# One layer's context products: a single run of tiled products per block, at another place in the block, with another cut of the features

## The chip, the cores and the metric

The kernel runs on one core of one Trainium2 chip. Times are device microseconds (us) of that core. "The trace" is the record of one profiled execution; "the page" is its summary. A stage's length below is read from the trace, from the start of the stage's first matmul to the start of the next stage's first.

## The reference, cut to what matters

128 sequences of 64 tokens with 768 features, two layers:

```python
h = jnp.maximum(_layernorm(x), 0.0)
for l in range(2):
    m_left  = einsum('bsh,oh->bso', h, W_left[l])       # pass one
    m_right = einsum('bsh,oh->bso', h, W_right[l])
    u       = ...                                       # scores from h, m_left, m_right, masked
    attention = exp(u) * adj / row sums
    h_lin = einsum('bsh,oh->bso', h, W_lin[l]) + b_lin[l]   # pass two
    ctx   = attention @ h_lin                               # the "context": 64x64 times 64x768
    h     = relu(layer_norm(ctx))
return x + h
```

Everything is in float32. In the trace each matmul of a product is two records on TensorE (the 8 matmuls of a context run, below, are 16 records).

## The kernel before: the parts concerned

Each layer has two passes over 16 blocks of 512 tokens (8 sequences). Pass one makes scores and attention. Pass two makes `h_lin` of block `u` as 15 products (ORDER has 15 entries; each product is 8 records of 256 columns), and, between two of them, the context of block `u-1`. A context product is 64x64, so four of them run at once on four quarters of TensorE ("tiled form"; in the trace the four start 6.6 ns apart). Results of products go to PSUM, the memory that TensorE writes; X, Y, Z, V and the two halves of each "aux" tile are its banks, of 512 columns each. `put(n, f)` sets step `f` of another engine into slot `n`; each product has two slots, in its middle and at its end.

```python
def context(u, r):                                   # half a block: 4 sequences
    cx = [ps_aux.tile([P, 2, T], F32, name="aux") for _ in range(2)]
    for n in range(2):
        for (j, k, i) in ((lo, 0, lo), (hi, 0, hi), (lo, 1, hi), (hi, 1, lo)):
            q = r + 2 * k
            m = n if j == lo else 1 - n              # the four tiles write four banks
            nc.tensor.matmul(cx[k][i, m, :HH], at[j, q, :], hl[j, q, m * HH:(m + 1) * HH], ...)
    return [c[:, :, :HH] for c in cx]                # HH = 384

def linear(u, rs, base, ends, more):
    for i, (s, at, t, _) in enumerate(ORDER):        # the 15 products
        ... matmuls into bank X, Y, Z or V; read(p, ...) by ScalarE or VectorE
        if i == 11 and more:
            AHEAD.append(fresh(l, 0, more))          # X for the next block, preloaded by ScalarE
        if i in ends:                                # a context run stands after product i
            what, slots = ends[i]
            for f, n in zip(finish(*what), slots):   # context + its layer norm, in later slots
                put(n, f)
...
if u:
    ends = {0: ((u - 1, 0), (6, 7, 8, 11, 12)), 7: ((u - 1, 1), (20, 21, 22, 30, 30))}
```

So before, the context of a block is two runs, after product index 0 and index 7 (the first and the eighth product), each of 8 matmuls of 384 columns (16 records). `finish` squares the context on ScalarE, then scales it by the inverse deviation; the last block of a layer works with half-width products (4 records).

## Time and profile before

| | before |
|---|---|
| time, median of 3 (range) | 2761.79 us (2761.58 to 2762.23) |
| span of the profiled execution | 2758.5 us |
| first layer: pass one, pass two | 897.49, 470.95 us |
| second layer: pass one, pass two to the end | 896.51, 480.21 us |
| period of a block in pass two, blocks 1 to 14 of both layers | 29.196 or 29.197 us (29.27 in block 1 of the second layer) |

The page, its chain and the blocks of pass two are shown in the prediction. This row of the page's costliest groups is every context record of the kernel (after the shapes: count, busy us, mean ns of one, idle time before):

```profile
L642 PE MATMUL aux<-hl,at 64*64 64x384 f32 x1024 | 99.2, 495 | 0.0
```

1024 records in groups of 16 are 64 runs: 32 blocks, two runs each. And these are four products of the last block of the first layer, TensorE in order of time (start, length by modelled ends, what; in brackets the idle time before it and who ended it):

```profile
1369.86 1.13 PE L758 MATMUL V<-w_n,ht 128*128 128x256 f32 x4
1370.83 1.03 PE L758 MATMUL X<-w_n,ts 128*128 128x256 f32 x4
1371.69 1.03 PE L758 MATMUL Y<-w_n,ts 128*128 128x256 f32 x4
1373.18 1.13 PE L758 MATMUL X<-w_n,ht 128*128 128x256 f32 x4 [0.47 <-ACT hl L200]
```

A product of four records normally takes 0.863 us from start to start (1370.83 to 1371.69). The one at 1371.69 takes 1.49: the next product waits for ScalarE to read a bank.

### The profile page before, as it was taken

The numbers are of one execution on the slowest core, as the hardware profiler recorded it, in microseconds if no ns is written. First come the engines' busy times: TensorE is split into PE (matmuls) and PEld (weight loads), VectorE is DVE, ScalarE is ACT, GpSimd is POOL, SyncE is SP. The second block draws the span as 40 slices with busy tenths as digits, with TensorE's granted clock in tenths as the row PEclk, the third lists the DMA queues.
The fourth block names the chain that finished last, engine by engine and source line by source line (L and its number), as shares of the span: only waits on it lengthen the run. The fifth ranks groups of instructions, "written<-read, shape, count | busy, mean of one in ns | idle before, by whom it ended". The sixth has DMA issues, their size and how long they took to land.

```text
span 2758.5 us, 46190 instructions
## 1 busy us (share of the span) xinstructions
PE 2731.5 (99%) x18712; PEld 2336.8 (85%) x18712; DVE 1333.8 (48%) x2255; ACT 842.3 (31%) x1469; POOL 1191.2 (43%) x935
## 2 busy tenths in 40 slices
PE   8999999999999999999999999999999999999998
PEld 7888888888888888888788888888888888888886
DVE  6555445544453322323335444443444335666667
ACT  3222223222321244444521211222121214544443
POOL 3332442223223465565422344223222335887886
PEclk9999999999999999999999999999999999999999
DMA  6424433343231343443545422443234204555555
GB/s 203 121 75 103 118 79 81 98 122 80 75 90 62 96 136 108 127 142 100 152 126 154 100 75 76 106 120 79 75 96 118 63 26 147 159 172 164 169 167 145
DMA packets 234070, 310.80 MB, mean 113 GB/s; under 512 B 54146, under 2 KB 184450, under 8 KB 225666
## 3 DMA queue, kind: packets, MB, share of 16 engines
q1 hardware_dynamic: 233698, 307.45, 40.3%
q8 instruction: 149, 2.44, 0.4%
q14 instruction: 63, 0.52, 0.1%
q10 hardware_dynamic: 160, 0.39, 0.0%
HBM read 202.91 MB, written 104.86 MB: 112 GB/s over the span
## 4 chain that ended last, share of the span: by engine, by line
PE 97%; DVE 1%; DMA 1%; ACT 0%; issue 0%; SPq 0%; DVEq 0%; ACTq 0%
PE X L422 23%; PE V L422 16%; PE X L758 12%; PE Y L422 12%; PE Z L422 8%; PE V L758 8%; PE Y L758 6%; PE aux L449 5%; PE Z L758 4%; PE aux L642 3%; DVE wm L463 0%; DMA w_l<-in_w_left_dram 0%; DMA w_r<-in_w_right_dram 0%; DVE w_l L155 0%; DVE w_r L155 0%
## 5 line engine op out<-in xcount | busy, mean ns | idle before, releaser
L155 POOL TENSOR_TENSOR ts<-ht 128x512 f32<-128x512 f32 x441 | 585.8, 1340 | 1218.3 <-DMA ht<-h 461.1
L200 ACT ACTIVATE m<-X 128x512 f32<-128x512 f32 (+1 forms) x256 | 151.6, 592 | 1101.0 <-PE X L422 583.7
L155 POOL TENSOR_TENSOR ts<-ht,ts 128x512 f32<-128x512 f32 x189 | 249.2, 1326 | 151.2 <-PE X L758 75.6
L155 DVE TENSOR_TENSOR m<-m,V 128x512 f32<-128x512 f32 (+1 forms) x256 | 173.3, 677 | 270.4 <-PE V L422 270.2
L155 DVE TENSOR_TENSOR m<-m,X 128x512 f32<-128x512 f32 (+1 forms) x256 | 162.9, 677 | 249.2 <-PE X L422 248.5
L758 PE MATMUL X<-w_n,ts 128*128 128x256 f32 x1024 | 244.1, 380 | 0.8 <-ACT hl L200 0.6
L422 PE MATMUL X<-ts,w_l 128*128 128x256 f32 x1024 | 242.7, 380 | 1.2 <-DVE ts L155 0.6
L422 PE MATMUL X<-ts,w_r 128*128 128x252 f32 (+1 forms) x1024 | 238.7, 376 | 0.0
L155 DVE TENSOR_TENSOR m<-m,Z 128x512 f32<-128x512 f32 (+1 forms) x128 | 87.4, 683 | 306.1 <-ACT m L200 246.6
L758 PEld LDWEIGHTS X<-w_n,ts 128*128 128x128 f32 x1024 | 191.6, 190 | 32.2 <-issue 2.3
L422 PEld LDWEIGHTS X<-ts,w_l 128*128 128x128 f32 x1024 | 192.0, 190 | 31.5 <-DVE m L155 2.7
L422 PEld LDWEIGHTS X<-ts,w_r 128*128 128x128 f32 x1024 | 192.0, 190 | 26.0
L268 ACT ACTIVATE ht<-ht,b_col,a_col 128x512 f32<-128x512 f32 x192 | 143.5, 804 | 135.9 <-DMA ht<-h 135.9
L758 PE MATMUL Y<-w_n,ts 128*128 128x256 f32 x768 | 182.5, 379 | 0.0
L422 PE MATMUL Y<-ts,w_l 128*128 128x256 f32 x768 | 181.5, 379 | 0.2 <-DVE w_l L155 0.2
L422 PE MATMUL Y<-ts,w_r 128*128 128x252 f32 (+1 forms) x768 | 179.2, 376 | 1.3 <-POOL w_r L155 1.3
L200 ACT ACTIVATE hl<-X 128x512 f32<-128x512 f32 (+1 forms) x136 | 77.7, 571 | 332.1 <-PE X L758 329.2
L758 PEld LDWEIGHTS Y<-w_n,ts 128*128 128x128 f32 x768 | 145.8, 190 | 20.4 <-issue 0.6
L422 PEld LDWEIGHTS Y<-ts,w_l 128*128 128x128 f32 x768 | 145.8, 190 | 20.3 <-DVE w_l L155 0.6
L422 PEld LDWEIGHTS Y<-ts,w_r 128*128 128x128 f32 x768 | 145.8, 190 | 19.1 <-POOL w_r L155 1.7
L155 DVE TENSOR_TENSOR hl<-hl,X 128x512 f32<-128x512 f32 (+1 forms) x136 | 83.1, 652 | 146.4 <-PE X L758 141.6
L155 DVE TENSOR_TENSOR hl<-hl,V 128x512 f32<-128x512 f32 (+1 forms) x136 | 89.0, 655 | 127.8 <-PE V L758 127.4
(143 smaller groups left out, 4701.1 us busy)
## 6 DMA issues: line engine op xcount, KB each, us to landing
ht<-h SPq DMA_DIRECT2D x63, 1536.0 KB, 7.2
h<-xb SPq DMA_DIRECT2D x124, 384.0 KB, 6.1
z<-z SPq DMA_DIRECT2D x128, 192.0 KB, 2.9
x<-z SPq DMA_DIRECT2D x128, 192.0 KB, 8.4
x<-in_x_dram SPq DMA_DIRECT2D x120, 192.0 KB, 8.4
xr<-in_x_dram SPq DMA_DIRECT2D x120, 192.0 KB, 3.6
out_dram<-xr SPq DMA_DIRECT2D x120, 192.0 KB, 2.6
adj<-in_adj_dram SPq DMA_DIRECT2D x64, 128.0 KB, 2.7
```

Source lines behind the costliest of these rows:

```text
L155: (eng.tensor_add if sign == "+" else eng.tensor_sub)(o, a, b)
L200: nc.scalar.activation(to(o), p, AF.Copy, scale=1.0 if sign == "+" else -1.0)
L268: nc.scalar.activation(ht, ht, AF.Relu, bias=cols[1][:, c:c + 1], scale=cols[0][:, c:c + 1])
L422: nc.tensor.matmul(p[:, g], w[ORDER[i][0]][:, c, g * P:(g + 1) * P], b()[t][:, c, :].rearrange(bs, s=S)[:, :, :ns], start=(new and g == c ...
L449: nc.tensor.matmul(p[h * S + e:h * S + e + 32, q, e:e + 95], ht[:, c, b * S + e:b * S + e + 32], mb[:, e:e + 95], start=(c == 0), stop=(c ...
L642: nc.tensor.matmul(cx[k][i, m, :HH], at[j, q, :], hl[j, q, m * HH:(m + 1) * HH], start=True, stop=True)
L758: nc.tensor.matmul(p[:, n], b[t][:, c, r * P:(r + 1) * P], w[s][:, c, :], start=(i in FIRST and i not in PRELOAD and n == c == 0), stop=(c ...
```

## The change

The intent: fewer changes between the ordinary and the tiled form. In the first layer, blocks 1 to 13, the whole context of a block is one run after product index 12, cut into 512 and 256 features instead of 384 and 384. It needs more PSUM than the two "aux" tiles hold, so banks X and Y serve too, and VectorE copies them out at once. Core of the diff (cuts marked with `...`):

```diff
+            def context_block(u):
+                aux = [ps_aux.tile([P, 2, T], F32, name="aux") for _ in range(2)]
+                x, y = (ps_st.tile([P, 2 * TH], F32, name=n) for n in "XY")
+                wide = {(1, 0): y, (1, 1): x, (0, 0): aux[0][:, 0], (0, 1): aux[0][:, 1]}
+                for r in (1, 0):
+                    for k in range(2):
+                        parts[r, k] = [wide[r, k], aux[1][:, k, r * D:(r + 1) * D]]
+                    for n, cut in enumerate((slice(0, T), slice(T, H))):       # 512, then 256
+                        for j, k, i in ((lo, 0, lo), (hi, 0, hi), (lo, 1, hi), (hi, 1, lo)):
+                            q = r + 2 * k
+                            nc.tensor.matmul(parts[r, k][n][i], at[j, q, :], hl[j, q, cut], start=True, stop=True)
+            def finish_block(u, more):
+                parts = context_block(u)
+                zs = {t: sp.tile([P, H], F32, name="z", bufs=4) for t in tiles}
+                for t in ((1, 1), (1, 0)):
+                    nc.vector.tensor_copy(zs[t][:, cut[0]], parts[t][0])       # X and Y out
+                    if t == (1, 1):
+                        AHEAD.append(fresh(l, 0, more))                        # X preloaded now
+                ... squares, deviation, inverse, scaled: per tile a 512 and a 256 part
+                for f, slots in ((squares, (25, 26, 28, 29)), (scaled, (33, 34, 35, 36))): ...
...
-                            "xb": ([P, H // 32, Q, 32], 1), "z": ([P, H], 3)}, ...
+                            "xb": ([P, H // 32, Q, 32], 1), "z": ([P, H], 4)}, ...
...
-                    if u:
+                    if u and last:
                         ends = {0: ((u - 1, 0), (6, 7, 8, 11, 12)), 7: ((u - 1, 1), (20, 21, 22, 30, 30))}
+                    elif u > NB - 3:
+                        ends = {5: ((u - 1, 0), (16, 17, 18)), 11: ((u - 1, 1), (28, 29, 30))}
+                    elif u:
+                        ends = {12: (u - 1, None)}
...
-                        ends = ({0: ((u - 1, 0), (12, 13, 15, 19, 21)), 11: ((u - 1, 1), (34, 35, 36, 42, 44))},
-                                {4: ((u, 0), (50, 51, 52, 56, 58))})
+                        ends = ({1: ((u - 1, 0), (13, 14, 16)), 11: ((u - 1, 1), (34, 35, 36))},
+                                {4: ((u, 0), (50, 51, 52))})
```

To make room for the fourth `z` buffer, the attention has two buffers instead of three and is loaded later, some constants move to a pool of pass one, and statistics pools shrink.

More of the change, by code (lines that the diff above doesn't have):

```diff
@@ L211 @@
     ATT = [[dram.tile([P, Q, S], F32, name=f"att{l}_{u}") for u in range(NB)] for l in range(L)]
-    ident = const.tile([P, P], F32, name="ident")
-    make_identity(nc, ident)
     eps_in = const.tile([P, 1], F32, name="eps_in")
@@ L219, with constants @@
     nc.gpsimd.memset(floor, 1e-30)
-    diff = const.tile([P, S], I32, name="diff")
     tri = const.tile([P, 2, S], F32, name="tri")
-    for h in range(PAIR):
-        r = slice(h * S, (h + 1) * S)
-        nc.gpsimd.iota(diff[r], pattern=[[-1, S]], base=0, channel_multiplier=1)
-    nc.vector.tensor_scalar(tri[:, 0, :], diff, 0.0, None, op0=ALU.is_le)
-    nc.vector.tensor_scalar(tri[:, 1, :], diff, 0.0, None, op0=ALU.is_gt)
+    KEEP = {}
+    def constants(pool):
+        KEEP["ident"] = pool.tile([P, P], F32, name="ident", bufs=1)
+        make_identity(nc, KEEP["ident"])
+        diff = pool.tile([P, S], I32, name="diff", bufs=1)
+        for h in range(PAIR):
+            r = slice(h * S, (h + 1) * S)
+            nc.gpsimd.iota(diff[r], pattern=[[-1, S]], base=0, channel_multiplier=1)
+        nc.vector.tensor_scalar(tri[:, 0, :], diff, 0.0, None, op0=ALU.is_le)
+        nc.vector.tensor_scalar(tri[:, 1, :], diff, 0.0, None, op0=ALU.is_gt)
     def mean_var(mv, halves):
-        st = stat.tile([P, 2, 6], F32, name="st")
+        st = stat.tile([P, 2, 6], F32, name="st", bufs=2)
         for n in range(2):
@@ L232, in mean_var @@
         nc.vector.bn_aggr(mv, st)
-    XR, KEEP = {}, {}
+    XR = {}
     START = (0, 2, 1, 3)
@@ L343, in turn @@
                         nc.tensor.transpose(p[:, c * P:(c + 1) * P],
-                                            xr[q][:, (3 * m + c) * P:(3 * m + c + 1) * P], ident)
+                                            xr[q][:, (3 * m + c) * P:(3 * m + c + 1) * P], KEEP["ident"])
                 for m, p in enumerate(banks):
@@ L491, in pass_one @@
             if l == 0:
+                constants(sp)
                 load_rows(0, 0, sp)
@@ L621, in pass_two, with load_at @@
             else:
-                places(sp, {"hl": ([P, Q, H], 2), "at": ([P, Q, S], 3), "x": ([P, 2, H], 2),
-                            "xb": ([P, H // 32, Q, 32], 1), "z": ([P, H], 3)}, ("hl", "at", "x", "xb", "z"))
+                places(sp, {"hl": ([P, Q, H], 2), "at": ([P, Q, S], 2), "x": ([P, 2, H], 2),
+                            "xb": ([P, H // 32, Q, 32], 1), "z": ([P, H], 4)}, ("hl", "at", "x", "xb", "z"))
             AT, HL = {}, {}
-            def load(u):
-                if (2, l, u) not in HT:
-                    load_h(2, l, u)
-                AT[u] = sp.tile([P, Q, S], F32, name="at", bufs=3)
+            def load_at(u):
+                AT[u] = sp.tile([P, Q, S], F32, name="at", bufs=2)
                 nc.sync.dma_start(AT[u], ATT[l][u])
@@ L644, in context @@
                 return [c[:, :, :HH] for c in cx]
+            def context_block(u):
+                hl, at = HL[u], AT[u]
+                lo, hi = slice(0, S), slice(S, P)
+                aux = [ps_aux.tile([P, 2, T], F32, name="aux") for _ in range(2)]
+                x, y = (ps_st.tile([P, 2 * TH], F32, name=n) for n in "XY")
+                wide = {(1, 0): y, (1, 1): x, (0, 0): aux[0][:, 0], (0, 1): aux[0][:, 1]}
+                parts = {}
+                for r in (1, 0):
[5 more added lines that the diff above has]
+                            nc.tensor.matmul(parts[r, k][n][i], at[j, q, :], hl[j, q, cut], start=True, stop=True)
+                return parts
             def batch(r, k, h):
@@ L677, in finish_last @@
                 xs = XS[u, r]
-                ss = [stat.tile([P, 1], F32, name="ss_e", bufs=2) for _ in range(2)]
-                rs = [stat.tile([P, 1], F32, name="sd_e", bufs=2) for _ in range(2)]
+                of = stat.tile([P, 2, 2], F32, name="of", bufs=1)
+                ss, rs = ([of[:, n, k:k + 1] for k in range(2)] for n in range(2))
                 for k in (1, 0):
@@ L698, in residual, with squares, deviation, inverse @@
                         nc.sync.dma_start(XS[u, r][k][h * S:(h + 1) * S], x[u * NBB + batch(r, k, h)])
+            def finish_block(u, more):
+                parts = context_block(u)
+                tiles = ((0, 0), (0, 1), (1, 0), (1, 1))
+                zs = {t: sp.tile([P, H], F32, name="z", bufs=4) for t in tiles}
+                cut = (slice(0, T), slice(T, H))
+                for t in ((1, 1), (1, 0)):
+                    nc.vector.tensor_copy(zs[t][:, cut[0]], parts[t][0])
+                    parts[t][0] = zs[t][:, cut[0]]
+                    if t == (1, 1):
+                        AHEAD.append(fresh(l, 0, more))
+                ss = stat.tile([P, Q, 2], F32, name="ssb", bufs=2)
+                sd = stat.tile([P, Q], F32, name="sdb", bufs=2)
+                rs = stat.tile([P, Q], F32, name="rsb", bufs=2)
+                def squares(t):
+                    junk = zs[0, t[1]]
+                    for n in range(2):
+                        nc.scalar.activation(junk[:, cut[n]], parts[t][n], AF.Square,
+                                             accum_out=ss[:, 2 * t[0] + t[1], n:n + 1])
+                def deviation():
+                    nc.vector.reduce_sum(sd, ss, axis=mybir.AxisListType.X)
+                    nc.scalar.activation(sd, sd, AF.Sqrt, bias=floor, scale=1.0 / (H - 1.0))
+                def inverse():
+                    nc.vector.tensor_scalar_add(rs, sd, EPS_LN)
+                    nc.vector.reciprocal(rs, rs)
+                def scaled(t):
+                    by = rs[:, 2 * t[0] + t[1]:2 * t[0] + t[1] + 1]
+                    for n in range(2):
+                        nc.scalar.activation(zs[t][:, cut[n]], parts[t][n], AF.Copy, scale=by)
+                    kept(u, *t, zs[t])
+                order = ((1, 1), (1, 0), (0, 0), (0, 1))
+                for f, slots in ((squares, (25, 26, 28, 29)), (scaled, (33, 34, 35, 36))):
+                    for n, t in zip(slots, order):
+                        put(n, lambda f=f, t=t: f(t))
+                put(30, deviation)
+                put(32, inverse)
@@ L700, in finish, with kept @@
+            def kept(u, r, k, z):
+                for h in range(PAIR):
+                    nc.sync.dma_start(ROWS[u][batch(r, k, h)], z[h * S:(h + 1) * S])
             def finish(u, r):
                 cx = context(u, r)
-                zs = [sp.tile([P, H], F32, name="z", bufs=4 if last else 3) for _ in range(2)]
+                zs = [sp.tile([P, H], F32, name="z", bufs=4) for _ in range(2)]
                 if last and not u and not r:
@@ L706, in finish @@
                 two = "p (n d) -> p n d"
-                ss = stat.tile([P, 2], F32, name="ss")
-                sd = stat.tile([P, 2], F32, name="sd1")
-                rs = stat.tile([P, 2], F32, name="rs1")
+                ss = stat.tile([P, 2], F32, name="ss", bufs=2)
+                sd = stat.tile([P, 2], F32, name="sd1", bufs=2)
+                rs = stat.tile([P, 2], F32, name="rs1", bufs=2)
                 for k in range(2):
@@ L729, in scaled @@
                         nc.scalar.activation(zs[k].rearrange(two, n=2), cx[k], AF.Copy, scale=rs[:, k:k + 1])
-                    for h in range(PAIR):
-                        nc.sync.dma_start(ROWS[u][batch(r, k, h)], zs[k][h * S:(h + 1) * S])
+                    kept(u, r, k, zs[k])
                 def done(k):
@@ L740, in done @@
                             residual(u + r, 1 - r)
-                return [inverse] + [lambda k=k: scaled(k) for k in range(2)] + [lambda k=k: done(k) for k in range(2)]
+                steps = [lambda f=f, k=k: f(k) for f in (scaled, done) for k in range(2)]
+                return [inverse] + (steps if last else steps[:2])
             def linear(u, rs, base, ends, more):
@@ L766, in linear @@
                         bank[FIRST[early[i]][0]] = fresh(l, early[i], rs)
-                    if i == 11 and more:
+                    if i == 11 and more and 12 not in ends:
                         AHEAD.append(fresh(l, 0, more))
@@ L770, in linear @@
                         what, slots = ends[i]
-                        for f, n in zip(finish(*what), slots):
-                            put(n, f)
+                        if slots:
+                            for f, n in zip(finish(*what), slots):
+                                put(n, f)
+                        else:
+                            finish_block(what, more)
                     run(base + 2 * i + 1)
-            load(0)
+            if (2, l, 0) not in HT:
+                load_h(2, l, 0)
             for u in range(NB):
                 turn = not last and u >= NB - 2
+                put(4, lambda u=u: load_at(u))
                 if u + 1 < NB:
-                    load(u + 1)
+                    load_h(2, l, u + 1)
                     put_all(9 if u else 15, affine(2, l, u + 1))
```

## The prediction

> **What bounds the kernel now.** I read four views in this order: the page (which engine), the chain of waits (what sets the end), TensorE's activity by stretches and in order of time in the first layer's second pass (what a block consists of), and the same for the last block of that layer.
>
> The page and its chain:
>
> ```profile
> span 2758.5 us, 46190 instructions
> PE 2731.5 (99%) x18712; PEld 2336.8 (85%) x18712; DVE 1333.8 (48%) x2255; ACT 842.3 (31%) x1469; POOL 1191.2 (43%) x935
> ...
> PE 97%; DVE 1%; DMA 1%; ACT 0%; issue 0%; SPq 0%; DVEq 0%; ACTq 0%
> ```
>
> TensorE is 99% busy, and 97% of the chain that ends last is TensorE; the other engines stand at 31 to 48%. So only what shortens TensorE's own stream, or one of its few stalls, can move the time. A busy TensorE is not a streaming one, though: ends of matmuls are modelled, so I go by starts.
>
> The stage the change touches, four consecutive blocks of the first layer's second pass (each row: the stretch, then its length and the busy time of each engine), and one such block in order of time:
>
> ```profile
> 939.15:968.35 29.20, 29.20 (x154) 23.59 (x153) 8.62 (x22) 14.05 (x25) 18.61 (x15) 1.00 0.39 117
> 968.35:997.54 29.19, 29.19 (x153) 23.59 (x152) 9.40 (x18) 12.83 (x24) 17.52 (x14) 1.00 0.55 186
> 997.54:1026.74 29.20, 29.20 (x153) 23.59 (x152) 8.55 (x16) 12.83 (x24) 17.58 (x15) 1.00 0.36 113
> ```
>
> ```profile
> 1079.86 1.89 PE L758 MATMUL Z<-w_n,ts 128*128 128x256 f32 x8
> 1081.59 1.89 PE L758 MATMUL V<-w_n,ts 128*128 128x256 f32 x8
> 1083.32 1.89 PE L758 MATMUL X<-w_n,ts 128*128 128x256 f32 x8
> 1085.13 1.52 PE L642 MATMUL aux<-hl,at 64*64 64x384 f32 x16
> 1086.59 1.99 PE L758 MATMUL Z<-w_n,ts 128*128 128x256 f32 x8
> 1088.42 1.89 PE L758 MATMUL X<-w_n,ts 128*128 128x256 f32 x8
> 1090.14 1.89 PE L758 MATMUL Y<-w_n,ts 128*128 128x256 f32 x8
> ```
>
> The block period is the same to 0.01 us each time, granted clock 1.00: no stall at all, a pure count of TensorE work. From start to start an ordinary product (8 records) takes 1.727 us (1081.59 to 1083.32), so one record of 256 columns is 1.727/8 = 0.2158 us. Around a context run the starts read 1.81 (product before it), 1.46 (the run), 1.83 (product after it). At the trace's full resolution these are 1.820, 1.451 and 1.831, and the two products are longer than 1.727 by 0.093 and 0.104. A context therefore occupies 0.093 + 1.451 + 0.104 = 1.648 us, and the block checks: 15 x 1.727 + 2 x 1.648 = 29.20.
>
> Inside the run, the weight loads show its steps:
>
> ```profile
> 1085.13 0.21 PEld L642 LDWEIGHTS aux<-hl,at 64*64 64x64 f32 x8 [0.33 <-issue]
> 1085.51 0.15 PEld L642 LDWEIGHTS aux<-hl,at 64*64 64x64 f32 x4 [0.17 <-issue]
> 1085.83 0.15 PEld L642 LDWEIGHTS aux<-hl,at 64*64 64x64 f32 x4 [0.17 <-issue]
> ```
>
> The 16 records go in four groups of four tiles that start 6.6 ns apart and run together. The groups start 0.373, 0.323, 0.322 us apart, and the fourth is followed by the next product after 0.431. A steady group of 384 columns is thus 0.3225 us (twice 384 columns at the rate of 0.2158 us for 256 gives 0.324, the same), and the bare streaming is 4 x 0.3225 = 1.290. The other 1.648 - 1.290 = 0.358 us is the price of going into the tiled form and out of it: 0.093 before, 0.050 in the first group, 0.109 after the last, 0.104 in the next product.
>
> **What the Trainium skill says.** "TensorEngine Tiling (Array Packing)", section Key Properties: changing the tiling mode drains TensorE, while changing tiles within a mode does not. The trace agrees: 0.358 us at every change of form and back, and next to nothing (2 to 3 ns) between groups within a run. "TensorE: Matmul & The Clock Gate", section The mechanism: tiles overlap, with starts some 4 ns apart; here 6.6 ns. The tiling page's Gotcha 1 (PSUM Pressure) says that different row tiles cannot use one PSUM bank simultaneously; the kernel before follows that, with its four tiles always in four banks, and the change does not (below), so no run yet shows whether it costs. "PSUM — Partial Sum Buffer", section PSUM bank collisions, tells that for engines the unit is bank and 32-partition quadrant together, and the two tiles in one bank of the change lie in different quadrants.
>
> **The change, part by part.** Blocks 1 to 13 of the first layer's second pass: two runs of context (after product 1 and product 8) become one after the 13th product. Blocks 14 and 15 keep separate runs at other places; the second layer's runs stay.
>
> Streaming: before, 2 runs x 4 groups x 0.3225 = 2.580 us a block. After, each half of the block has two groups of 512 columns and two of 256: 4 x 0.429 (twice 512 columns at 0.2158 for twice 256, less the 2.5 ns or so that a record costs beyond its columns) + 4 x 0.2158 = 2.580. Nothing gained. Weight loads: four of 133 ns overlap (0.15 us for four), and fit under the short group's 0.216. No stall from them.
>
> Changes of form: two pairs become one, 0.358 us saved a block, so 29.20 becomes 28.84. Over 13 blocks: 13 x 0.358 = 4.65 us.
>
> Added off TensorE: VectorE copies two 512-wide parts out of the banks X and Y (an addition of that size takes 0.68 us, so about 1.3 us a block; VectorE is busy 8.6 of 29.2). ScalarE's squares and scalings go from 8 instructions of 768 wide to 16 of 512 or 256; with 0.49 us from start to start for 512 and some 0.28 for 256, plus the reading of the sum (about 0.1), four tiles cost some 3.9 us of squares and 3.1 of scalings. ScalarE stands at 12.8 of 29.2, so it has room, and this layer has no other work for it there. All beside TensorE if the deadlines hold. Counting from the run's start: its last group ends at 2.74, product 14 begins there, then product 15, and the next block's first product, which needs X, begins at 6.30. The X tile is complete at about 1.0, copied by VectorE by 1.8, X preloaded by ScalarE at 2.5: 3.8 us to spare. Squares run from 2.5 to about 6.4, the deviation follows, and ScalarE is free by the read of the first product at 8.2. The scalings stand around the read of the third product, due by 13.2: the read of the second ends near 10.5, two scalings at 0.8 take it to 12.1, the read ends at 12.7. Half a microsecond to spare, the tightest place. The run itself waits for Y's read, which VectorE ends about 0.9 us after product 12, with product 13 (1.73) lying between.
>
> The last block: z gets four buffers instead of three. In the kernel before, a square waits there for a store of z:
>
> ```profile
> 1370.93 0.81 ACT L711 ACTIVATE z<-aux 128x768 f32<-128x768 f32 x1 [0.66 <-DMA z<-z]
> ```
>
> and shortly after, one product of four records takes 1.49 us from start to start where 0.86 is usual. I take 0.65 us back from it. The context run that waits 0.78 us (start to start 2.23 for 1.45) for its bank keeps its place and its wait. The moved constants, the smaller statistics pools and the later loads of the attention are off the path: nothing.
>
> Sum: 4.65 + 0.65 = 5.3 us; 2761.8 - 5.3 = 2756.5.
>
> **The rivals.** (1) Two row tiles in one bank take turns. For it: the tiling page, and that the kernel before keeps them apart. Against: different quadrants. If so the groups take twice as long: +2.58 us a block, +33.5 in all, less 4.65: about 2790. I give it 4%. (2) A wait takes the place of the drain: X or Y not free in time, or ScalarE late for the third product's read because of the scalings. Spare is 0.5 us at the tightest place, and ScalarE instructions of 256 are only an estimate. If it misses by 0.2 us in each of 13 blocks, 2.6 us go: 2759. I give it 15%. (3) The last two blocks, whose runs move by some products, stall more or less than before by a microsecond: 2755.5 to 2757.5. (4) The entry and exit cost is not fixed but grows with the banks and semaphores of the first group (it now waits for a load and VectorE at once): a tenth of a microsecond a block, 1.3 us.
>
> **Range and chances.** Main case 2756.5; half of (2) and (4) upward, (3) and a better last block downward, and 0.65 us of spread in the measured times: 2754.8 to 2758.8. Even rival 1 is +1.0%, so within 2% is 0.98; faster by over 2% would need 55 us, more than all of the change of form costs in the whole kernel (64 runs x 0.358 = 23 us): 0.005. Slower by over 2%: 0.015.
>
> **What would show it.** The block period in the first layer's second pass should be 28.84 us instead of 29.20, with one context run of 32 records of about 2.74 us from its start to the next product, groups at 0.43 and 0.22 us, entry 0.09 and exit 0.10. If groups read 0.86 and 0.43, rival 1 is right. If the products after the run read over 1.73, above all the first or the fifth of the next block, rival 2. If the waits of squares on z's store are gone from the last block but its length is not, my 0.65 is wrong. The prediction fails if the block period does not fall by 0.3 to 0.4 us.

## The result, and the profile after

| | before | after |
|---|---|---|
| time, median of 4 runs each, same chip (range) | 2761.68 us (2759.47 to 2762.23) | 2755.03 us (2753.41 to 2756.92) |
| ratio (95% interval) | | 0.9978 (0.9960 to 0.9995) |
| span of the profiled execution | 2758.5 | 2755.1 |

Ratios here are the mean time of one kernel's runs over that of the other's of the same rounds, so not quite the ratio of the medians. A ratio of 0.9978 is a gain of 0.0022 x 2761.68 = 6.1 us; a second batch (below) gave 0.9983, 4.7 us. The prediction was a gain of 5.3 and a time of 2756.5 in a range of 2754.8 to 2758.8.

The page and its chain, after:

```profile
span 2755.1 us, 46372 instructions
PE 2726.7 (99%) x18712; PEld 2339.0 (85%) x18712; DVE 1349.0 (49%) x2268; ACT 850.0 (31%) x1612; POOL 1192.1 (43%) x935
...
PE 96%; DVE 1%; DMA 1%; ACT 1%; issue 0%; SPq 0%; DVEq 0%; ACTq 0%
```

TensorE has the same number of records (18712) and 4.8 us less of busy time. VectorE and ScalarE have 15.2 and 7.7 us more, but in the chain they stand at 1% each, no more than in the second trace of the kernel before (2 and 1%). Two whole blocks of the first layer's second pass (stretch; length; busy us and count of TensorE, its weight loads, VectorE, ScalarE and GpSimd; granted clock; DMA share and GB/s):

```profile
962.43:991.27 28.84, 28.84 (x153) 23.75 (x152) 9.79 (x19) 14.73 (x36) 15.22 (x12) 1.00 0.42 131
991.27:1020.11 28.84, 28.84 (x153) 23.75 (x153) 9.83 (x17) 13.45 (x35) 17.68 (x14) 1.00 0.36 115
```

The period fell from 29.20 to 28.84, in all 13 blocks alike (28.838 or 28.839). The context of one block, TensorE in order of time, answers to the block shown in the prediction:

```profile
987.73 1.89 PE L830 MATMUL Y<-w_n,ts 128*128 128x256 f32 x8
989.45 1.89 PE L830 MATMUL V<-w_n,ts 128*128 128x256 f32 x8
991.27 0.65 PE L668 MATMUL Y<-hl,at 64*64 64x512 f32 x2
991.29 0.65 PE L668 MATMUL X<-hl,at 64*64 64x512 f32 x2
991.75 0.59 PE L668 MATMUL Y<-hl,at 64*64 64x512 f32 x2
991.77 0.60 PE L668 MATMUL X<-hl,at 64*64 64x512 f32 x2
992.18 1.90 PE L668 MATMUL aux<-hl,at 64*64 64x256 f32 x24
994.01 1.99 PE L830 MATMUL Z<-w_n,ts 128*128 128x256 f32 x8
995.84 1.89 PE L830 MATMUL V<-w_n,ts 128*128 128x256 f32 x8
```

The first two groups, of 512 columns, start at 991.27 and 991.75 and are followed at 992.18: 0.48 (the first group pays the entry) and 0.43 us. From the run's start to the next product it is 2.74 us, and the products on its two sides take 1.82 and 1.83. The weight loads show the groups after them:

```profile
992.18 0.58 PEld L668 LDWEIGHTS aux<-hl,at 64*64 64x64 f32 x12 [0.28 <-issue]
993.04 0.15 PEld L668 LDWEIGHTS aux<-hl,at 64*64 64x64 f32 x4 [0.28 <-issue]
993.47 0.15 PEld L668 LDWEIGHTS aux<-hl,at 64*64 64x64 f32 x4 [0.28 <-issue]
```

Three groups (two of 256 columns, one of 512) start in the 0.86 us from 992.18 to 993.04: 2 x 0.216 + 0.43. The next group of 512 again takes 0.43 (to 993.47).

Where the time went by stages, in two traces of each kernel:

| stage, us | before | before again | after | after again |
|---|---|---|---|---|
| up to pass one's first product | 13.31 | 13.31 | 13.92 | 14.46 |
| first layer, pass one | 897.49 | 898.14 | 899.44 | 899.07 |
| first layer, pass two | 470.95 | 470.96 | 466.16 | 466.16 |
| second layer, pass one | 896.51 | 895.21 | 894.33 | 894.49 |
| second layer, pass two | 480.21 | 480.85 | 481.30 | 480.34 |
| span | 2758.5 | 2758.5 | 2755.1 | 2754.5 |

The changed stage repeats to 0.01 us and is 4.79 shorter. Every other stage moves by up to 2.2 us from kernel to kernel, and by up to 1.3 from trace to trace of one kernel, although its work was not meant to change. (The start was: the constants moved into pass one, and in all 12 traces of kernels with the change's edits it takes 13.5 to 14.5 us.) That is not small beside the gain, and it is why a total alone cannot tell this change's parts apart. The experiments are therefore read by stage as well as by total.

### The profile page after: what moved, and what is told of

It is laid out like the page before. It is cut to its first block, busy times and chain, and to the rows that moved or that the text cites. A ratio compares the mean times of both kernels' runs of the same rounds, so it can differ in the third digit from the quotient of the medians.

```text
span 2755.1 us, 46372 instructions
## 1 busy us (share of the span) xinstructions
PE 2726.7 (99%) x18712; PEld 2339.0 (85%) x18712; DVE 1349.0 (49%) x2268; ACT 850.0 (31%) x1612; POOL 1192.1 (43%) x935
## 4 chain that ended last, share of the span: by engine, by line
PE 96%; DVE 1%; DMA 1%; ACT 1%; issue 0%; SPq 0%; DVEq 0%; ACTq 0%
PE X L426 23%; PE V L426 16%; PE X L830 12%; PE Y L426 12%; PE Z L426 8%; PE V L830 8%; PE Y L830 6%; PE aux L453 5%; PE Z L830 4%; PE aux L645 2%; PE aux L668 1%; PE Y L668 0%; ACT ht L272 0%; DMA w_r<-in_w_right_dram 0%; DMA ht<-h 0%
## 5 line engine op out<-in xcount | busy, mean ns | idle before, releaser
L796 POOL TENSOR_TENSOR z<-z,b 128x768 f32<-128x768 f32 x62 | 112.0, 1817 | 79.7 <-DVE z L793 79.7
```

The lines of the kernel that those rows point to most:

```text
L796: nc.gpsimd.tensor_add(zs[k], zs[k], rows["b"])
```

## The experiments

Theory: the whole gain in steady blocks is one pair of changes of form less, 0.358 us a block, wherever the runs stand and however they are cut; the rest is in the last block. Rival A: the gain comes with the other edits (fourth `z` buffer, later loads, other places of the runs). Rival B: the cut of 512 and 256, or the banks X and Y, costs or saves something by itself. Rival C: the total is what it is for reasons of the untouched stages.

| run | what | time, us (range; runs) | ratio to before (95%) | first layer, pass two, us |
|---|---|---|---|---|
| e0_after | the change again | 2755.15 (2754.16 to 2756.66; 5) | 0.9983 (0.9970 to 0.9995) | 466.16 |
| e1_split2 | block run in two pieces | 2761.15 (2759.39 to 2762.59; 5) | 1.0003 (0.9990 to 1.0015) | 470.81 |
| e2_split3 | in three pieces | 2764.94 (2764.55 to 2767.50; 4) | 1.0019 (1.0005 to 1.0033) | 475.98 |
| e3_rest | all but the block run | 2762.12 (2761.25 to 2763.89; 5) | 1.0007 (0.9993 to 1.0020) | 471.66 |
| f1_rest_z3 | e3 with three `z` buffers | 2766.99 (1 run, state unknown) | | 475.52 |
| f2_move | change + last block's first run one product later | 2756.21 (2754.88 to 2757.12; 4) | 0.9981 (0.9965 to 0.9998) | 465.44 |
| g_all | block run in blocks 14 and 15 too | 2761.76 (2760.05 to 2762.70; 4) | 1.0002 (0.9987 to 1.0017) | 471.01 |
| b0_before | before again | 2760.25 (1 run, state unknown) | | 470.96 |
| h_both to h4_both | block run in the second layer too | below | | |

### The change again, beside its cuts: e0, e1, e2, e3

> The changed kernel again, unchanged, as the yardstick of this batch. Theory A (the gain is the form changes of TensorE saved): 5 to 6 us under the kernel before, block period 28.84 us in the first layer's second pass. Theory B (the gain came from the other edits: z buffers, later loads, moved runs of the last blocks): same time here, but the other runs of the batch tell.

The first run repeats the changed kernel on the chip that ran the next three, so that their differences are those of one batch: 2755.15, and 466.16 us in the stage, the same to the hundredth as in the first trace.

> The one run a block is cut in two (the second half half-way through the 14th product), the rest of the change kept. Theory A: one more entry and exit a block, so the block period goes from 28.84 back to 29.20 us and the time up by 13 x 0.358 = 4.65 us. Theory B: period and time stay as in the changed kernel.

The edit gives back one pair of changes of form and nothing else: same matmuls, same banks, same copies, but the second half of the run is put half a product later (and the first square one slot).

```diff
-                return parts
+                def piece(r, n): ...             # the four matmuls of one half and one cut
+                return parts, piece
...
+                piece(1, 0); piece(1, 1)
+                put(26, lambda: piece(0, 0), lambda: piece(0, 1))
-                for f, slots in ((squares, (25, 26, 28, 29)), ...
+                for f, slots in ((squares, (26, 26, 28, 29)), ...
```

One block of it by stretches, then the run in its two pieces:

```profile
991.27:1020.47 29.20, 29.20 (x156) 23.57 (x152) 9.83 (x17) 13.57 (x35) 17.69 (x15) 1.00 0.35 113
```

```profile
991.38 0.61 PE L670 MATMUL aux<-hl,at 64*64 64x256 f32 x8
991.92 1.13 PE L836 MATMUL Z<-w_n,ts 128*128 128x256 f32 x4
992.98 1.52 PE L670 MATMUL aux<-hl,at 64*64 64x512 f32 x16
994.43 1.13 PE L836 MATMUL Z<-w_n,ts 128*128 128x256 f32 x4
```

Half a product (4 records) stands between the pieces; it takes 1.06 us (991.92 to 992.98) instead of 0.863, which is one exit and one entry (0.104 + 0.093). The period is 29.20 again, and the stage 470.81: 4.65 us more than the change, which is 13 x 0.358 to the hundredth.

> The same run cut in three. Theory A: period 28.84 + 2 x 0.358 = 29.56 us, time up by 9.3 us over the changed kernel, above the kernel before. Theory B: no change. If the period rises by clearly less than 0.358 for each cut, the entry cost isn't fixed but depends on the place or on the size of the groups.

```diff
+                piece(1, 0)
+                put(26, lambda: piece(1, 1))
+                put(27, lambda: piece(0, 0), lambda: piece(0, 1))
```

The run in its three pieces:

```profile
993.12 1.13 PE L836 MATMUL Z<-w_n,ts 128*128 128x256 f32 x4
994.18 0.66 PE L670 MATMUL aux<-hl,at 64*64 64x256 f32 x8
994.77 1.13 PE L836 MATMUL Z<-w_n,ts 128*128 128x256 f32 x4
995.83 1.52 PE L670 MATMUL aux<-hl,at 64*64 64x512 f32 x16
```

Both halves of the product take 1.06 us. Two steady blocks take 59.11 us, so one takes 29.56, which is 28.84 + 2 x 0.358. The stage is 475.98: 9.82 us more than the change, where 2 x 4.65 = 9.30 was due; the rest is two products after the first block's run that take 0.44 and 0.08 us more, once. So a steady block grows in equal steps with the count of changes of form, and totals follow in the same order: 2755.15, 2761.15, 2764.94.

> Everything of the change except the one run a block: all blocks keep two runs (after the 6th and the 12th product). Theory A: block period 29.20 us, time within 1 us of the kernel before (0.65 less by my estimate for z's fourth buffer). Theory B: as fast as the changed kernel.

Everything of the change but the block run: all blocks keep two runs.

```diff
-                    elif u > NB - 3:
-                        ends = {5: ((u - 1, 0), (16, 17, 18)), 11: ((u - 1, 1), (28, 29, 30))}
                     elif u:
-                        ends = {12: (u - 1, None)}
+                        ends = {5: ((u - 1, 0), (16, 17, 18)), 11: ((u - 1, 1), (28, 29, 30))}
```

```profile
1013.30:1042.50 29.20, 29.20 (x154) 23.60 (x153) 8.85 (x17) 12.80 (x25) 19.31 (x16) 1.00 0.37 113
```

The block is 29.20 us, and the time is 2762.12: nothing of the gain is left, so rival A falls. (The stage is 0.71 us longer than before: at the new places products wait once in block 1 and once in block 14, 0.54 and 0.31 us with what follows them, and the last block is 0.14 shorter. These belong to this run's places of the runs, so of the 5.50 us between it and the change 4.65 are the change of form.) With 384-wide runs at other places (e3) and with 512 and 256 in two pieces (e1), the period is the same 29.20: the cut and the banks neither cost nor save, so rival B falls. What makes up the 0.358 us inside TensorE, the drain itself or the first weight loads of the other form, no run here separates.

### The last block: f1, f2, g

> The run without the one run a block again, but z with three buffers as in the kernel before: only the last block of the first layer matters, in the trace. If the fourth buffer is what took away the late square there, it waits for a store of z again (some 0.66 us) and the product of four records that took 1.49 us in the kernel before takes 1.4 to 1.5 again instead of 0.86. If the buffer had nothing to do with it, that product stays at 0.86.

This is e3 with `z` back at three buffers (`bufs=4` to `bufs=3` in the first layer). The stage is 475.52, 3.86 us longer than e3. ScalarE's squares wait for stores of `z` again, and TensorE then waits for ScalarE (one row of each, ScalarE and TensorE in order of time):

```profile
1356.18 0.81 ACT L783 ACTIVATE z<-aux 128x768 f32<-128x768 f32 x1 [1.43 <-DMA z<-z]
```

```profile
1357.73 1.39 PE L830 MATMUL X<-w_n,ht 128*128 128x256 f32 x4 [1.99 <-ACT hl L200]
```

Further on, the product that took 1.49 in the kernel before takes 1.55. So the fourth buffer is what takes that stall away, as the prediction said, and with the runs at these places it is worth more than 0.65. But in the change the gain does not arrive. After the change, earlier in the last block (TensorE, then ScalarE's read that the second row waits for):

```profile
1348.23 1.03 PE L830 MATMUL Y<-w_n,ts 128*128 128x256 f32 x4
1349.71 1.13 PE L830 MATMUL X<-w_n,ht 128*128 128x256 f32 x4 [0.45 <-ACT hl L200]
```

```profile
1349.29 0.36 ACT L200 ACTIVATE hl<-X 128x256 f32<-128x256 f32 x1
```

Here a product takes 1.48 us from start to start: 0.62 too many. The run after product index 1 puts two squares (0.81 us each) on ScalarE just ahead of the read of X. The old stall of 0.63 went and a new one of 0.62 came; the last block went from 35.67 to 35.53 us, so the stage gained 4.79 = 4.65 + 0.14, not 5.30.

> The changed kernel, the first run of context in block 15 after its third product instead of its second. If the new stall there (1.48 us for the product to Y where 0.86 is usual) comes from ScalarE doing two squares between the third product and its read, the read now comes before the squares and the stall goes: the first layer's second pass 0.6 us shorter, total 0 to 1 us less (below the spread). If the stall comes from something else, it stays at 0.6.

```diff
-                        ends = ({1: ((u - 1, 0), (13, 14, 16)), 11: ...
+                        ends = ({2: ((u - 1, 0), (15, 16, 17)), 11: ...
```

One product later, the same two products read:

```profile
1348.89 1.13 PE L830 MATMUL Y<-w_n,ts 128*128 128x256 f32 x4
1349.86 1.03 PE L830 MATMUL X<-w_n,ht 128*128 128x256 f32 x4
```

0.97 us is 0.863 + 0.104 of the exit from the run ahead of it: no stall. The stage is 465.44, the shortest of all: 0.72 less than the change, and 5.51 less than before, near the 5.30 that the prediction had for it. The 0.72 is the stall of 0.62 and 0.10 in the product after it: a product after such a stall takes 0.104 more (0.967 for 0.863), just as one after a context run does. So this part of the price is not peculiar to the change of form. In total, 2756.21 and a ratio of 0.9981 cannot be told from the change's 0.9978 and 0.9983: 0.7 us is below the spread. By the trace it is the best version; by the clock it is not shown to be.

> One run a block for the last two blocks too (all 15 that have a next block). By TensorE's count 2 x 0.358 = 0.7 us less, and the stall of the moved run (0.6) gone: up to 1.3 us under the changed kernel. Rival: with products of half the size ScalarE is behind in block 15, and stalls there take the 0.7 back or more.

The block run in blocks 14 and 15 too:

```diff
-                        ends = ({1: ((u - 1, 0), (13, 14, 16)), 11: ((u - 1, 1), (34, 35, 36))},
-                                {4: ((u, 0), (50, 51, 52))})
+                        ends = ({12: (u - 1, None)}, {6: ((u, 0), (54, 55, 56))})
```

```profile
1368.67 1.13 PE L830 MATMUL X<-w_n,ht 128*128 128x256 f32 x4 [2.20 <-ACT hl L200]
```

The stage is 471.01: all of the gain is given back in the last block. Its products are half as wide, so ScalarE has half the time between two reads for the same squares and scalings, and TensorE waits for it five times (1.1, 0.7, 1.5, 2.4 and 1.3 us). That is why the change leaves these two blocks with separate runs.

### The second layer too: h, h2, h3, h4

The second layer's blocks have the same two pairs of changes of form. If rate alone counted, the same edit would save another 4.65 us there.

> One run a block in the second layer too, for its blocks 1 to 13. By TensorE's count the block period there goes from 29.20 to 28.84 us and the time down by another 4.65 us, to about 2750.5. Rival: GpSimd, busy 28.5 of 29.1 us a block in that layer before, or VectorE, which gets two copies and six more instructions a block, is late; then the period stays at 29.2 or rises, and the products show waits for VectorE or for the sums of GpSimd.

```diff
+                def scaled_last(t): ...      # VectorE: context x 1/deviation x a; GpSimd: + b
+                def done(t): ...             # VectorE: max(z, 0) + x; store
-                for f, slots in (... (scaled, (33, 34, 35, 36))):
+                for f, slots in (... (scaled, (33, 34, 35, 36))) + (((done, (38, 40, 42, 44)),) if last else ()):
...
-                    if u and last:
-                        ends = {0: ((u - 1, 0), (6, 7, 8, 11, 12)), 7: ((u - 1, 1), (20, 21, 22, 30, 30))}
+                    if u > NB - 3 and last:
+                        ends = {5: ..., 11: ...}          # other blocks as in the first layer
```

2783.57 us (2780.77 to 2785.28, 4 runs), ratio 1.0080 (1.0065 to 1.0095), and 507.89 us in the second layer's second pass, whose steady block rises to 30.8 us. I had looked to GpSimd, the busiest after TensorE there. The trace names VectorE (TensorE, VectorE and GpSimd at one time in a steady block):

```profile
2379.24 1.99 PE L852 MATMUL X<-w_n,ts 128*128 128x256 f32 x8 [1.72 <-DVE hl L155]
```

```profile
2374.07 3.92 DVE L770 SCALAR_TENSOR_TENSOR xr<-z,xr 128x768 f32<-128x768 f32 x2
```

```profile
2375.19 3.93 POOL L155 TENSOR_TENSOR ts<-ht 128x512 f32<-128x512 f32 x2
```

Two last steps (`xr<-z,xr`) take 3.92 us on VectorE, ahead of its reads of `hl` that free the banks. In the kernel before, one such step takes 0.95 or 0.96 us where no GpSimd instruction is under way at its start (two of 60). The other 58 began while one was, and each of the 58 ended 0.811 to 0.819 us after that instruction's end. "SBUF — State Buffer" of the Trainium skill, section Who interferes with whom, says that a VectorE instruction with two SBUF inputs contends with GpSimd's reads, and speaks of an exclusive lock, not a slowing; the trace agrees: what is left after the other's end is always the same and no more than a step takes alone, so these steps wait rather than run slower.

Ahead of more of them, one look at the kernel before, to see which of its stage lengths repeat:

> The kernel before once more, for a second trace of it. Open after the traces so far: the first layer's first pass reads 897.5 us in the one trace of the kernel before and 898.5 to 900.9 in the traces of the kernels that carry the change, with one wait of 1 to 1.9 us at about 76 us that the profile gives no releaser for. If that belongs to the change, this trace shows 897.5 again and no such wait; if it is spread between executions, it may show one.

The changed stage does, 470.96, and so do two stalls (the product of 1.49 us, and one of 0.69 us too long in the first block of the second layer's first pass, on which more below). The other stages are in the table above.

In three more runs VectorE's steps are spread over more slots, and the last blocks return to separate runs in other ways; f2's move is in all three. Ratios are to the kernel before of the same batch.

> One run a block in both layers, the moved run of block 15, and in the second layer VectorE's scalings and last steps spread to one a product, in products where it has few reads. If the 1.87 us stall of the first try in the second layer was only VectorE's four last steps standing together ahead of its reads, the block period there is 28.84 and the time about 2750 to 2752; if VectorE or GpSimd has no room at all in that layer, stalls stay and the period is 29.2 or more.

```diff
-(scaled, (33, 34, 35, 36))   (done, (38, 40, 42, 44))
+(scaled, (33, 35, 37, 41))   (done, (39, 43, 45, 49))
```

> As the last try, whose steady blocks in the second layer took 28.89 us but whose blocks 14 and 15 lost some 13 us because TensorE waited for VectorE to free the context's banks. Here one run a block ends one block earlier, and blocks 13 and 14 take their two runs at later places, so that VectorE catches up. If only the change-over was wrong: second layer's second pass 476 to 479 us (480.2 to 481.3 in the other kernels), time 2 to 4 us under the changed kernel. If VectorE has no room for what was put off, the stalls move to blocks 13 to 15 and the time stays at or above the changed kernel's.

```diff
+                    if u == NB - 3 and last:                # change over one block earlier
+                        ends = {7: ((u - 1, 0), (20, 21, 22, 30, 31)), 13: ((u - 1, 1), (32, 33, 34, 38, 40))}
+                    elif u == NB - 2 and last:
+                        ends = {5: ((u - 1, 0), (16, 17, 18, 22, 24)), 11: ((u - 1, 1), (27, 28, 29, 34, 36))}
```

> The last try with one edit: in the second layer's block 14 the two runs stand after the 4th and the 10th product instead of the 6th and the 12th, so that GpSimd gets the two additions ahead of its last sums and VectorE's last steps do not wait for it. If that wait (3.4 us of the last try's stalls, with some 2 us after it) was the rest of the change-over, the second layer's second pass takes 478 to 480 us instead of 484.75, and the time is 2 to 4 us under the changed kernel (about 2752 to 2754). If the lateness only moves to another place, it stays at 482 or more and the second layer is better left alone.

```diff
-                        ends = {5: ((u - 1, 0), (16, 17, 18, 22, 24)), 11: ((u - 1, 1), (27, 28, 29, 34, 36))}
+                        ends = {3: ((u - 1, 0), (12, 13, 14, 16, 18)), 9: ((u - 1, 1), (23, 24, 25, 32, 34))}
```

| run | time, us (range; 5 runs each) | ratio (95%) | second layer, pass two, us |
|---|---|---|---|
| h2_both | 2764.29 (2763.10 to 2765.93) | 1.0007 (0.9993 to 1.0021) | 490.26 |
| h3_both | 2759.22 (2757.31 to 2760.48) | 0.9984 (0.9971 to 0.9998) | 484.75 |
| h4_both | 2758.14 (2756.10 to 2758.37) | 0.9986 (0.9973 to 1.0000) | 482.69 |

In h2 the first separate run after the block runs waits 2.8 us for VectorE, and in h3, after it, a product waits 3.2 us for VectorE; each next run was made to end the longest such wait. Spread out, the steps let the steady block of the second layer run at 28.89 us, against 29.20 (28.84 was expected). The return to separate runs at the end is what costs. In h4 block 13, block 14 and the first half of block 15 take 29.42, 31.61 and 19.56 us, against 29.20, 29.20 and 17.75 in the change (16.79 in its second trace): 4.4 to 5.4 us more, where blocks 1 to 12 save 3.6 in all. The first block, which has no context run, is 0.55 longer; it also differs by 0.65 between the two traces of the kernel before. The second layer stays at 482.69, above the 480.3 to 481.3 of the change, so leaving it alone was right for these arrangements; that no arrangement could do it is not shown.

## Why the prediction was right, point by point

- **The change of form, 13 x 0.358 = 4.65.** Right. The period is 28.84 in all 13 blocks, and e1 adds exactly 4.65 back. The terms were right too: entry 0.093 and 0.05, groups 0.429 and 0.216, run 2.74, product after it 1.83. (The 2.5 ns that the prediction takes off a group follow from its own lengths: 0.2158 - 2 x (0.3225 - 0.2158) is 0.0024 us for a record of no columns.)
- **Slips of its text.** Its four parts of 0.358 add up to 0.356 as rounded, and it speaks of four blocks and prints three. Its 23 us for all changes of form leaves out the 32 score runs of pass one, which are in a tiled form too (128x32) and have products of 1.82 and 1.83 us beside them as well. Its conclusion, that 55 us are out of reach, is not touched.
- **Rival 1, two row tiles in one bank take turns.** Refuted: groups would read 0.86 and 0.43, and read 0.43 and 0.22. Of the two pages that the prediction weighs here, the PSUM page's unit, bank and quadrant together, is the one that fits.
- **Rival 2, a wait in place of the drain.** It did not come, but the margin was smaller than said. ScalarE around the third product's read:

```profile
1001.72 0.71 ACT L758 ACTIVATE z<-z,rsb 128x512 f32<-128x512 f32 x1
1002.33 0.47 ACT L758 ACTIVATE z<-aux,rsb 128x256 f32<-128x256 f32 x1
...
1003.65 0.60 ACT L200 ACTIVATE hl<-X 128x512 f32<-128x512 f32 x1
```

  The squares took what was predicted (3.9 us), but two tiles' scalings took 1.93 us (1001.72 to 1003.65), not 1.6. The read ended 12.98 us after the run's start instead of 12.7, and was due at 13.2: 0.2 us to spare, not 0.5. The term that was mis-sized is the scaling: from start to start it takes 0.61 for 512 columns and 0.36 for 256, where 0.49 and 0.28 had been put.
- **Rival 4, a dearer entry.** No: 0.093 and 0.05 as before.
- **The last block, 0.65.** This step was right in its mechanism (the fourth buffer ends the wait for the store, as f1 shows by taking it away) and wrong as a term of the sum: a new wait of 0.62 us from the moved run took its place, and the stage got 0.14. The prediction had named this sign itself ("If the waits of squares on z's store are gone from the last block but its length is not, my 0.65 is wrong"). The profile still puts one wait of a square there down to a store, 1.02 us in the change, but that square begins 0.10 us after the run that it reads has ended, as the same one does in the kernel before, so the store holds nothing up. Rival 3 had allowed for it ("more or less than before by a microsecond"). f2 recovers it.
- **The total.** It came out at 2755.03, within the range by 0.23 us; the two batches' intervals allow a gain of 1.4 to 11.0 and of 1.4 to 8.3 us, so the total alone does not show that the gain is 5.3. 4.79 us are shown in the changed stage. The rest of the difference, in either direction, comes from stages whose work did not change, and was not in the sum. Two parts of it have a place in the traces. First, in the first block of the second layer's first pass, one product took 0.69 us longer in both traces of the kernel before, 0.66, 0.69 and 0.51 in e3, f1 and g, and under 0.04 in the change (both traces), e1, e2, f2 and the four h runs. In the traces of before and after, the first step of the inverse deviation on VectorE takes 0.89 us before and 0.22 after; it ends each time as a GpSimd sum ends, so it is a matter of how the two fall together, and luck for the change. Second, against the change: in all 12 traces of kernels that carry its edits, the first product after the first scores of pass one (after the first of 32 runs of 192 short matmuls) takes 0.8 to 1.8 us more than the 1.83 of the kernel before, as here in the repeated run:

```profile
78.35 1.24 PE L426 MATMUL Z<-ts,w_l 128*128 128x256 f32 x5 [1.16 <-issue]
```

  In neither trace of the kernel before is it there. It is in e3 and f1 too, so it comes neither from the block run nor from the fourth buffer. The profile names no releaser ("issue"), and no experiment was made on what is left (the moved constants, the statistics pools, the attention's loads): its cause is open.

  The traces say more of such waits. Score runs take 4.057 us or, in 8 to 13 of the 32 of each trace, of the kernel before too, up to 1.0 us more. Number TensorE's instructions in the trace (matmuls, weight loads and the few others) from 0 in order of time: in all 14 traces each of these waits, and the one above, ends at a number that is 193 or 194 past a multiple of 256 (149 of 149), and only where that is matmul 150 or later of the run or stands just behind it. So they belong to places in TensorE's stream of instructions and not to the data of one stage; why one is long here and short there was not tested (the wait above is at number 961, which the kernel before passes without one). With these waits taken out, the first layer's pass one is 895.1 to 895.5 us in all 14 traces: nearly all of its spread from 897.5 to 900.9 is theirs.

  In this sense rival C holds for the last microsecond or two: the stage gave 4.8, and that the total came out near 5.3 is these differences falling as they did.

## What to carry to other kernels

Where TensorE is busy for the whole span, count what is not streaming: here a change between forms of matmul had a fixed price (0.358 us there and back), read off the starts on both sides of a run, and joining runs saved that price times their number. Before moving work off such a run, look at the queue of the engine that must free the banks for it, above all in blocks that are narrower than the others: that is where the joined run lost all it had gained (g), and where a place one product later was worth 0.7 us (f2). When a change is worth 0.2%, read its stage in the trace, because untouched stages vary by as much.

## What the Trainium skill lacked or had wrong

- "TensorEngine Tiling (Array Packing)", Key Properties, says that a change of tiling mode drains TensorE, and gives no cost. The runs show 0.358 us for going in and out (0.093 in the product before, 0.050 in the first group, 0.109 after the last, 0.104 in the next product), the same for runs of 8, 16 and 32 records, and additive (e1, e2). The last part, 0.104, also follows a stall without a change of form (f2).
- The same page, Gotcha 1 (PSUM Pressure), says that different row tiles cannot use one PSUM bank simultaneously. Here two row tiles write one bank in different quadrants at the full rate (0.429 us for 512 columns, 0.216 for 256, where taking turns would double both), with correct results. (For the page that fits, see rival 1 above.)
- No page that I found gives a length for the waits without a releaser that the traces show in runs of 192 short matmuls and just after the first: up to 1.0 us in a run, 0.8 to 1.8 after the first, all at instructions 193 or 194 past a multiple of 256. The cause is open.
